# An eight-layer network on one core: one table of constants, two products of each attention unit on GpSimd, and the last step of the norms on ScalarE

## The chip, the cores and the metric

The kernel runs on one core of a Trainium2 chip. The time is device time in microseconds, the median of three runs. All arithmetic is in 32-bit floats, apart from some small bf16 operands of TensorE.

## The reference, cut to what matters

Four sequences of 1024 tokens with 128 features pass through eight layers. Each is `x = layernorm(x + layer(x))`, with mean and variance over the 128 features of a token:

- layer 0: cosine similarities within a sequence of 1024, counted and fed through a small map
- layer 1: a dense network whose weights are first binarised (sign times a mean)
- layer 2: an attention in each token between its 16 heads' channels; it is the largest part
- layer 3: a dense network with ternary weights and an inner norm
- layer 4: a gated linear recurrence; layer 5: four nested experts; layer 6: a state-space layer
- layer 7: a top-2 mixture of Kronecker-factored experts, whose tables are gathered by index

Layer 2 as the kernel computes it, for each token and head, with 64 channels as queries q, keys k and values v, and a running maximum m: `e = exp(q*k - m)`, summed over the keys a query may see, and `e*v` summed in the same way; the quotient is the output.

## The kernel before, in words

**Tiling.** The 4096 tokens are 32 tiles of 128 (`T`), in eight blocks of four tiles. For layers 3 to 7 the last block is split into two groups of two tiles, which makes nine groups (`SIZES`). Each tile gives layer 2 two *units* of 64 tokens, 64 units in all. A unit is laid out so that four partitions share the keys of a token, and its queries `qr` and maxima `mr` are copied into that layout by DMAs from SP's queue, issued in `prepare` (line 758). `qr` and `mr` have two buffers each.

**A unit of attention** is 17 pieces of e, which `feed` (line 817) starts in the order d1, n8 to n14, d0, n0 to n7. Piece nK has 32 x (60 - 4K) columns (n0 1920, n3 1536, n8 896), and d0 and d1 have 1024 each: 17408 columns a unit. Each piece takes room in a ring of 8768 columns (`ERING`), is handed out in order, and goes through six steps:

1. VectorE (DVE): e = q * k, with q from `qr` in SBUF and k from `kvr` in PSUM (in `feed`)
2. GpSimd (POOL): e = e - m (in `rest`, line 857)
3. ScalarE (ACT): e = exp(e)
4. TensorE (PE): sums of e into `acc` (`add_up(0)`)
5. DVE: e = e * v, in place, v from `kvr` in PSUM
6. PE: sums of e * v into `acc` (`add_up(1)`), after which the ring's room is free

`close` (line 910) turns `acc` into the layer's output and norm, once a unit.

**The other layers** run beside this. `chain_a` runs layers 0 and 1 (`front`, line 1710) of two blocks, then layers 3, 4 and 5 group by group, with the layers 0 and 1 of later blocks between; `chain_b` runs layer 6, `chain_c` layer 7. `norm` (line 528) ends layers 0, 1, 3, 4, 5 and 6: `stats` takes mean and variance on DVE and the reciprocal deviation `rs` on ACT, then one `tensor_scalar` on DVE for each tile of 128 columns reads PSUM and writes x; after it PE transposes x and ACT copies the transpose. It is called 52 times, for 192 tiles. Layer 2's norm is in `close` and layer 7's in `layer7`; both have code of their own.

**The order.** Each engine works through its instructions in the order in which they are written. That order is not in the source: every piece of work is a generator that says on which engine its next step goes and what it needs, and `Order` (line 109) picks the next step by a model of costs (`length`, line 65) and by ranks (`URGE`). A step of the other layers goes ahead of the attention's, unless its chain is ahead of its due place (`urge`, `LAG`). All instructions go through a recording helper, so all of them have line 52 in the profile and are told apart by tiles.

**The start.** `start` (line 382) loads 33 small constants and parameters by 37 DMAs, all on SP's queue, then `w0`, the biases and `Wo`. `fold` then loads layer 2's weights and folds a centring matrix `less` into them on PE and ACT. `layer0` of blocks 0 and 1 does `normalise` and `count` for both blocks together; `binarise` (line 622) comes next and writes layer 1's weights to DRAM scratch; then layer 1 of block 0, and with it the first unit can be prepared.

Of the kernel before, what the change touches and what calls it, by code (L numbers as in the profile page):

```python
# [14 lines left out]
AF = mybir.ActivationFunctionType  # L15
ALU = mybir.AluOpType
# [4 lines left out]
P = 128  # L21
NB, SEQ, D = 4, 1024, 128
NG = 8
TPG = 4
# [6 lines left out]
SH = S * H  # L31
ERING = 8768
LUMPS = 8
EPS = 0.05
ONE = 96
LAG = {"chain_a": (0.7, 300), "chain_b": (1.6, 290), "chain_c": (2.6, 132)}
# [249 lines left out]
class Model:  # L286
# [95 lines left out]
    def start(self):  # L382
        nc, a = self.nc, self.a
        load = {"ident": P, "rep": P, "SL": P, "U": P, "ex4": P, "ex2": P, "g4": 16, "g2": 32, "su": P, "sd": P, "par": 4, "iota": LUMPS,
                "blk": P, "less": P, "bz": 48, "route": 16, "beyond": R}
        par = {"f0_b1": 4, "f1_lnw": 4, "f1_lnb": 4, "a2_nw": 1, "f2_b1": 16, "f2_Wu": 1, "a0_W1": 1, "a0_b1": 1}
        wide = {"f2_bu": 1, "a3_bdt": 16, "a3_Alog": 16, "f3_sup": 1, "f3_sdn": 1}
        total = sum(load.values()) + sum(par.values()) + sum(wide.values()) + 64 + 32 + 128
        cst = self.keep([P, total], "cst")
        self.k, at = {}, 0  # L390

        def put(name, src, cols, bcast=False, rows=P):
            nonlocal at
            dst = cst[:, at : at + cols]
            self.k[name] = dst
            at += cols
            for r in range(0, P, rows):
                self.d.dma_start(dst[r : r + rows], src.to_broadcast([P, cols]) if bcast else src)

        put("ident", a["c_ident"], P)  # L400
        self.ident = self.k["ident"]
# [5 lines left out]
        self.v.memset(self.eps, LN_EPS)  # L407
        for g in (0, 1):
            self.load_x(g)
        for n, c in par.items():  # L410
            put(n, a[n], c)
        for n, c in load.items():
            if n != "ident":
                put(n, a["c_" + n], c)
        for n, c in wide.items():
            put(n, a[n], c, bcast=True)
        put("bup", a["f3_bup"], 64, rows=64)
        put("bdn", a["f3_bdn"], 32, rows=32)
        put("bd", a["c_bd"], 128)
        self.w0 = self.keep([P, 2, D], "w0")  # L420
# [107 lines left out]
    def norm(self, g, c, r):  # L528

        x = g.x  # L530
        mv, rs = yield from self.stats(r, c)
        for j in range(g.n):
            self.v.tensor_scalar(x[:, j, :], r[:, j, :], mv[:, j, 0:1], rs[:, j : j + 1], ALU.subtract, ALU.mult)
        self.drop(r)
        yield from self.transpose(g.xT, [x[:, j, :] for j in range(g.n)])
# [70 lines left out]

    def layer0(self, b):
        gs = self.blocks[2 * b : 2 * b + 2]
        for g in gs:
            if g.x is None:  # L610
                yield "SP", self.free("x")
                self.load_x(g.k)
            yield "ACT", self.free("xT")
            g.xT = self.new("xT")
        yield "ACT", self.free("ha")
        nT = self.new("ha")
        yield from self.together(*(self.normalise(g, nT) for g in gs))
        yield from self.together(*(self.count(g, nT) for g in gs))
        self.drop(nT)


    def binarise(self):

        self.w1 = []
        for half, n, count in ((0, 1, D), (1, 4, 512)):
# [24 lines left out]
            yield "SP"  # L650
            self.w1.append(self.keep([P, 512], "w1", pool=self.dram))
            self.d.dma_start(self.w1[half], wT)
            self.drop(wT)
# [52 lines left out]
    def fold(self):  # L706

        flat = self.Wkv.rearrange("p r v h n -> p (r v h n)")  # L710

        def piece(w, name, at):
            raw = yield from self.load("a", self.a[name][:, at : at + 512])
            yield "PE", self.free("bg")
            ps, dst = self.new("bg"), w[:, at : at + 512]
            self.pe.matmul(ps, lhsT=self.k["less"], rhs=raw, start=True, stop=True)
            yield "ACT"
            self.s.copy(dst, ps)
            self.drop(raw, ps)
            yield "SP"  # L720
            self.d.dma_start(dst[ONE : ONE + 1], self.a[name + "_b"][:, at : at + 512])

        yield from self.together(
            *(piece(w, name, at) for w, name, n in ((self.Wq, "a1_Wq", 2), (flat, "a1_Wkv", 4)) for at in range(0, 512 * n, 512))
        )
        self.folded = self.order.latest

# [30 lines left out]
    def prepare(self):  # L758

        flat = lambda tt: tt.rearrange("p h c -> p (h c)")  # L760
        for T in range(NG * TPG):
# [13 lines left out]
            for u in range(2):  # L775
# [12 lines left out]
                unit["uses"] = [9, 8]  # L788
                unit["subs"] = 17
                unit["ready"] = True  # L790
# [26 lines left out]
    def feed(self):  # L817
# [5 lines left out]
        count = 0  # L823
        for unit in self.units:
            for kind, i in order:
# [13 lines left out]
                else:  # L839
# [5 lines left out]
                    shape = lambda tt, nq=nq: tt.rearrange("p (a q) -> p a q", q=nq)  # L845
                yield "DVE", self.when(lambda: self.ering.can(SH * nq), lambda: self.ering.back(SH * nq)), True
                et = self.ering.take(SH * nq)
                e = shape(et)
                self.v.tensor_tensor(e, part(unit["qr"]), kk, ALU.mult)
                what = dict(first=(kind, i) == order[0], last=(kind, i) == order[-1], q0=q0, nq=nq, half=half)  # L850
                rest = self.rest(unit, count, kind, et, shape, part(unit["mr"]), vv, **what)
                self.order.spawn(rest, "rest", self.order.latest)
                count += 1
            self.drop(unit["qr"])
        self.retire("qr", "big", "a", "c")

    def rest(self, unit, count, kind, et, shape, m, vv, first, last, q0, nq, half):
        e = shape(et)
        rows = et.rearrange("p (s h q) -> p s h q", s=S, q=nq)

        def add_up(d):
            for hb in range(2):
                for s in range(S):
# [4 lines left out]
                    )  # L868

        yield "POOL"  # L870
        self.g.tensor_tensor(e, e, m, ALU.subtract)
# [838 lines left out]
    def front(self, b):  # L1710
        if b.k % 2 == 0:
            yield from self.layer0(b.k // 2)
        if b.k == 0:
            yield from self.binarise()
        yield from self.layer1(b)
# [62 lines left out]
    def run(self):  # L1778
# [13 lines left out]
        with self.tc.manual_schedule():  # L1792
            self.log_exp()
            self.order.spawn(self.fold(), "feed")
            self.order.spawn(self.prepare(), "prepare")
            for chain in (self.chain_a, self.chain_b, self.chain_c):
# [3 lines left out]
        assert not self.held and all(len(self.slots[k]) >= n for k, (n, _) in self.room.items()), self.slots  # L1800


URGE = {"close": 0, "prepare": 1, "chain_a": 2, "chain_b": 2, "chain_c": 2, "rest": 3, "feed": 4}
# [9 lines left out]
def arrays_of(i):  # L1813
# [63 lines left out]
    for n, s in (("up", "up"), ("dn", "down")):  # L1877
# [9 lines left out]
        "U": p <= q,  # L1887
        "rep": p % 32 == q % 32,
        "blk": (p % 16 == q % 16) / 8.0,
        "less": ((p == q) * 1.0 - (p == ONE)) * (q != ONE),  # L1890
        "bz": np.pad(p // 8 == np.arange(16)[None, :], ((0, 0), (16, 16))) * 8**-0.5,
# [11 lines left out]
    }  # L1903
    a.update({"c_" + n: c(np.asarray(v, np.float32)) for n, v in k.items()})
    return a
# [17 lines left out]
```

## Time and profile before

| | before |
|---|---|
| median of three runs | 4459.69 us (4457.38 to 4463.85) |
| the profiled execution's own time | 4459.83 us |
| its span, first to last instruction | 4458.1 us |
| DVE busy in the span | 3637.0 us |
| PE busy | 3532.0 us |
| POOL busy | 2697.3 us |
| ACT busy | 2443.8 us |
| first product of a unit on DVE starts at | 135.42 us |
| last product e * v of the last unit on DVE starts at | 3998.78 us |

The span falls into three stages: a start of 135 us, a long stage to about 4000 us in which the 64 units and the other layers run side by side, and an end of 458 us in which the layers of the last groups finish alone. "Busy" is the time in which an engine had an instruction in work; the idle time ahead of a group of instructions is put down to what ended last before it. A mean duration can count overlap with the next instruction; busy time divided by the count does not.

### The profile page before, as it was taken

The numbers are of one execution on the slowest core, as the hardware profiler recorded it, in microseconds if no ns is written. First come the engines' busy times: TensorE is split into PE (matmuls) and PEld (weight loads), VectorE is DVE, ScalarE is ACT, GpSimd is POOL, SyncE is SP. The second block draws the span as 40 slices with busy tenths as digits, with TensorE's granted clock in tenths as the row PEclk, the third lists the DMA queues.
The fourth block names the chain that finished last, engine by engine and source line by source line (L and its number), as shares of the span: only waits on it lengthen the run. The fifth ranks groups of instructions, "written<-read, shape, count | busy, mean of one in ns | idle before, by whom it ended". The sixth has DMA issues, their size and how long they took to land.

```text
span 4458.1 us, 91232 instructions
## 1 busy us (share of the span) xinstructions
PE 3532.0 (79%) x37044; PEld 1856.1 (42%) x37044; DVE 3637.0 (82%) x5143; ACT 2443.8 (55%) x4083; POOL 2697.3 (61%) x1254
## 2 busy tenths in 40 slices
PE   4567677788788888888788888988788888879973
PEld 2222224344344434444354434544354434437762
DVE  2899999899888998879979998779989998883421
ACT  3455555766446755657555655657555654555520
POOL 0598866776567775567756766557666775560111
PEclk8788889988899989989899888999998988998976
DMA  1221212212223232222323333133323223331555
GB/s 52 67 57 39 47 42 61 50 44 50 58 65 79 73 95 67 67 72 67 96 64 86 77 87 84 38 84 87 89 60 96 67 74 86 77 89 34 142 153 124
DMA packets 389933, 328.12 MB, mean 74 GB/s; under 512 B 201660, under 2 KB 325372, under 8 KB 389512
## 3 DMA queue, kind: packets, MB, share of 16 engines
q1 hardware_dynamic: 379016, 288.73, 26.3%
q0 software_dynamic: 10496, 33.56, 2.6%
q8 instruction: 290, 4.75, 0.5%
q14 instruction: 131, 1.07, 0.1%
HBM read 147.05 MB, written 40.89 MB: 42 GB/s over the span
## 4 chain that ended last, share of the span: by engine, by line
DVE 37%; PE 31%; issue 12%; POOL 9%; ACT 9%; DMA 2%; SPq 1%; DVEq 0%; POOLq 0%; ACTq 0%
DVE ringe L52 23%; PE bg L52 18%; PE acc L52 10%; POOL ringe L52 9%; DVE bg L52 5%; ACT ringe L52 4%; PE kvr L52 3%; SPq L52 1%; DVE a L52 1%; DVE x L52 1%; ACT ha L52 1%; DVE b L52 1%; DVE ast L52 1%; DVE t L52 1%; ACT b L52 1%
## 5 line engine op out<-in xcount | busy, mean ns | idle before, releaser
L52 POOL TENSOR_TENSOR ringe<-ringe,mr 128x1024 f32<-128x1024 f32 (+14 forms) x1088 | 2548.7, 2380 | 1150.5 <-DVE ringe L52 789.9
L52 PE MATMUL acc<-ringe,cst 128*32 128x256 f32 (+6 forms) x17418 | 1370.6, 428 | 509.2 <-ACT ringe L52 244.3
L52 ACT ACTIVATE ringe<-ringe 128x256 f32<-128x256 f32 (+14 forms) x962 | 997.6, 1053 | 790.2 <-POOL ringe L52 788.1
L52 DVE TENSOR_TENSOR ringe<-ringe,kvr 128x1024 f32<-128x1024 f32 (+14 forms) x1098 | 1289.8, 1204 | 129.9 <-PE acc L52 108.2
L52 DVE TENSOR_TENSOR ringe<-qr,kvr 128x1024 f32<-128x1024 f32 (+14 forms) x1088 | 1278.4, 1211 | 82.3 <-PE acc L52 45.7
L52 PEld LDWEIGHTS acc<-ringe,cst 128*32 128x32 f32 x17418 | 424.5, 115 | 1230.7 <-DVE ringe L52 467.6
L52 ACT ACTIVATE ringe<-ringe,cst 128x256 f32<-128x256 f32 x512 | 353.5, 771 | 106.7 <-POOL ringe L52 106.1
L52 PE MATMUL bg<-xT,a 128*128 128x512 f32 (+2 forms) x506 | 286.9, 675 | 34.8 <-DVE t L52 11.1
L52 PEld LDWEIGHTS bg<-b,b 64*128 64x128 f32 (+1 forms) x1650 | 178.8, 203 | 101.3 <-issue 42.6
L52 PE MATMUL bg<-b,b 64*128 64x128 f32 (+2 forms) x1650 | 202.2, 290 | 18.9 <-DVE b L52 5.5
L52 PE MATMUL kvr<-wkv,xT 128*32 128x256 f32 x2048 | 157.1, 430 | 48.4 <-DVE ringe L52 48.0
L52 PE MATMUL bg<-a,ha 128*128 128x128 f32 x1168 | 169.5, 291 | 12.8 <-ACT ha L52 12.8
L52 DVE TENSOR_TENSOR_SCAN bg<-lo,bg 128x512 f32<-128x512 f32 x128 | 155.4, 1217 | 22.2 <-ACT bg L52 22.2
L52 ACT COPY b<-bg 128x512 f32<-128x512 f32 (+2 forms) x245 | 106.7, 446 | 121.7 <-PE bg L52 119.8
L52 PEld LDWEIGHTS bg<-a,ha 128*128 128x128 f32 x1168 | 149.9, 201 | 24.9 <-ACT ha L52 14.5
L52 PEld LDWEIGHTS bg<-xT,a 128*128 128x128 f32 (+1 forms) x506 | 92.1, 213 | 159.1 <-issue 62.0
L52 ACT ACTIVATE ha<-bg,cst 128x512 f32<-128x512 f32 (+1 forms) x157 | 102.2, 665 | 79.8 <-PE bg L52 78.2
L52 POOL DMA_INDIRECT c<-in_f_tdn,elumps x22 | 20.8, 943 | 200.4 <-issue 196.0
L52 ACT ACTIVATE bg<-bg 128x512 f32<-128x512 f32 (+3 forms) x176 | 89.2, 509 | 75.8 <-PE bg L52 73.3
L52 ACT ACTIVATE b<-cst,five 128x128 f32<-128x128 f32 x412 | 129.5, 392 | 0.0
L52 DVE TENSOR_TENSOR b<-b,bg 128x256 f32<-128x256 f32 (+3 forms) x272 | 100.9, 401 | 34.0 <-PE bg L52 18.3
L52 PE MATMUL bg<-b,cst 128*128 128x512 f32 (+1 forms) x208 | 113.9, 634 | 0.5 <-ACT b L52 0.4
(598 smaller groups left out, 4641.5 us busy)
## 6 DMA issues: line engine op xcount, KB each, us to landing
qr<-q SPq DMA_DIRECT2D x512, 128.0 KB
mr<-t SPq DMA_DIRECT2D x512, 128.0 KB
a<-in_f_W SPq DMA_DIRECT2D x65, 256.0 KB
c<-in_f_Wdn SPq DMA_DIRECT2D x55, 256.0 KB
tu<-c SPq DMA_DIRECT2D x52, 256.0 KB
c<-tu SPq DMA_DIRECT2D x200, 64.0 KB
c<-td SPq DMA_DIRECT2D x98, 128.0 KB
td<-c SPq DMA_DIRECT2D x47, 256.0 KB
```

The costliest lines, as they stand in the source:

```text
L52: return f(*args, **kw)
```

## The change

**One table.** The constants and small parameters are laid side by side on the host in one array of 1475 columns, which two DMAs load: the identity matrix first, then the rest. The matrix `less` is loaded by `fold` on its own and given back.

**The order of the start.** `binarise` is a task of its own from the beginning; layer 1 waits until both its weights are written. `layer0` of the first pair still normalises both blocks, but counts only block 0; block 1's count comes when `chain_a` reaches block 1.

**Two shared products.** For pieces n8 and n3 of each unit, step 1 goes to POOL: ACT copies the 32 columns of k from PSUM to a small tile `ks` in SBUF, POOL multiplies q by it, and then subtracts m as before. `qr` is given back when the last of the 17 products is done, on whichever engine (`asked`).

**The last step of the norms.** In `norm`, DVE makes `nm = -mean * rs` from two small SBUF tiles (one `scalar_tensor_tensor` of up to four columns), and ACT applies scale and bias, one `activation` for each tile of 128 columns.

```diff
 def start(self):
-        load = {...}; par = {...}; wide = {...}
...
-        for n, c in par.items():
-            put(n, a[n], c)
...
-        put("bd", a["c_bd"], 128)
+        cst = self.keep([P, sum(CST.values())], "cst")
+        for name, cols in CST.items():
+            self.k[name] = cst[:, at : at + cols]
+            at += cols
+        self.load_x(0)
+        self.d.dma_start(cst[:, :P], a["cst"][:, :P])
+        self.load_x(1)
+        self.d.dma_start(cst[:, P:], a["cst"][:, P:])
...
 def norm(self, g, c, r):
         mv, rs = yield from self.stats(r, c)
+        nm = self.small([P, TPG], c + "nm")[:, : g.n]
+        self.v.scalar_tensor_tensor(nm, mv[:, :, 0], -1.0, rs, ALU.mult, ALU.mult)
+        yield "ACT"
         for j in range(g.n):
-            self.v.tensor_scalar(x[:, j, :], r[:, j, :], mv[:, j, 0:1], rs[:, j : j + 1], ALU.subtract, ALU.mult)
+            self.s.activation(x[:, j, :], r[:, j, :], AF.Identity, scale=rs[:, j : j + 1], bias=nm[:, j : j + 1])
...
 def layer0(self, b):
+        room = "ha" if b else "hc"
...
         yield from self.together(*(self.normalise(g, nT) for g in gs))
+        if b == 0:
+            yield from self.count(gs[0], nT)
+            return nT
         yield from self.together(*(self.count(g, nT) for g in gs))
...
 def feed(self):
-                yield "DVE", self.when(lambda: self.ering.can(SH * nq), lambda: self.ering.back(SH * nq)), True
+                shared = (kind, i) in SHARED
+                yield "ACT" if shared else "DVE", self.when(
+                    lambda: self.ering.can(SH * nq), lambda: self.ering.back(SH * nq)
+                ), True
...
-                self.v.tensor_tensor(e, part(unit["qr"]), kk, ALU.mult)
+                qk = part(unit["qr"]), kk
+                if shared:
+                    ks = self.small([P, SH], "ks", bufs=4)
+                    self.s.copy(ks, kk[:, :, 0])
+                    qk = qk[0], ks[:, :, None].to_broadcast(sh)
+                else:
+                    self.v.tensor_tensor(e, *qk, ALU.mult)
+                    self.asked(unit)
...
+    def asked(self, unit):
+        unit["asks"] -= 1
+        if unit["asks"] == 0:
+            self.drop(unit["qr"])
+            if unit is self.units[-1]:
+                self.retire("qr", "big", "a", "c")
...
 def rest(...):
+        if qk:
+            yield "POOL"
+            self.g.tensor_tensor(e, *qk, ALU.mult)
+            self.asked(unit)
         yield "POOL"
         self.g.tensor_tensor(e, e, m, ALU.subtract)
...
 def front(self, b):
         if b.k % 2 == 0:
-            yield from self.layer0(b.k // 2)
-        if b.k == 0:
-            yield from self.binarise()
+            self.nT = yield from self.layer0(b.k // 2)
+        elif b.k == 1:
+            yield from self.count(b, self.nT)
+            self.drop(self.nT)
+        yield "SP", self.when(lambda: len(self.w1) == 2)
         yield from self.layer1(b)
...
 def run(self):
+            self.w1 = []
+            self.order.spawn(self.binarise(), "chain_a")
...
+SHARED = ("n", 8), ("n", 3)
```

## The prediction

> **What bounds the kernel now.** I read first the busy times, then the same by stage, then the chain that ended last, then who waits for whom, and last the groups by shape.
>
> ```profile
> span 4458.1 us, 91232 instructions
> PE 3532.0 (79%) x37044; PEld 1856.1 (42%) x37044; DVE 3637.0 (82%) x5143; ACT 2443.8 (55%) x4083; POOL 2697.3 (61%) x1254
> ...
> DVE 37%; PE 31%; issue 12%; POOL 9%; ACT 9%; DMA 2%; SPq 1%; DVEq 0%; POOLq 0%; ACTq 0%
> ```
>
> The same in three stages (after the stage and its length: busy us of PE, PEld, DVE, ACT, POOL, then clock, DMA share, GB/s):
>
> ```profile
> 0.00:135.00 135.00, 69.52 (x258) 39.43 (x258) 35.20 (x93) 48.70 (x107) 3.41 (x9) 0.82 0.24 62
> 135.00:4000.00 3865.00, 3121.37 (x32117) 1546.01 (x32117) 3465.59 (x4567) 2242.98 (x3563) 2642.32 (x1189) 0.89 0.28 70
> 4000.00:4458.00 458.00, 341.11 (x4677) 270.61 (x4669) 136.21 (x485) 152.14 (x413) 51.53 (x56) 0.77 0.43 110
> ```
>
> In the long middle stage DVE is busy 3466 of 3865 us, 90%; PE 81%, POOL 68%, ACT 58%. DVE leads. What its 399 idle us wait for, and whom POOL waits for:
>
> ```profile
> DVE ringe L52 <- PE acc L52: 157.2, 126, 9.8
> DVE ringe L52 <- PE kvr L52: 39.3, 27, 3.5
> POOL ringe L52 <- DVE ringe L52: 789.9, 158, 20.4
> ```
>
> So POOL is fed by DVE and has room; PE is the engine that DVE waits for. DVE work taken out of this stage should shorten it, as far as PE lets it. Start and end are chains of short steps in which no engine is full.
>
> **The change, part 1: the start.** The chain in the start, in order of time:
>
> ```profile
> 21.70 4.20 DMA a<-in_a_Wq
> 25.95 5.46 PE bg L52 x10
> 35.48 12.84 PE bg L52 x40
> 87.83 5.67 PE bg L52 x8
> 135.43 1.21 DVE ringe L52
> ```
>
> The first weight is issued at 21.70 because 44 DMAs stand before it on SP's queue, 0.47 us each. In the changed order 11 stand before it: 0.74 + 11 x 0.47 = 5.9, and 4.2 to land gives 10.1 us. But the bytes ahead of it grow denser (some 2.5 MB; the stretch 4200 to 4300 moved 179 GB/s at a DMA share of 0.68, so 263 GB/s at full share, 9.5 us). I take 12.5: gain 13.4 us.
>
> From the first similarity product (36.94 in the timeline) to layer 1's first (87.83) are 50.9 us: the similarities of two blocks, then the binarising from 68.95 on. Afterwards there are 8 products of 0.86 us (6.9), then block 0's own steps, read off the same stretch: count 1.1, map on DVE 0.8, softplus on ACT 2.4 and DVE 0.7, PE 3.4, sum and statistics 2.3, deviation 0.6, norm 2.1, transposes 1.4, copy 0.6, with hops some 16.8. Together 23.7, gain 27.2. The binarising is costed at nothing: it took 18.9 us, starts at about 20 on the new scale and is hidden by these steps until about 47; were it late, layer 1 would wait for it.
>
> Block 1's count now lies between layer 1 of block 0 and the first unit, where block 1's layer 1 lay before (47.6 us in all): I charge 3 us. Sum: 13.4 + 27.2 - 3 = 37.6; the first product comes at 98 instead of 135.4. Some 8 us of DVE work of block 1 move into the middle stage.
>
> **Part 2: two products.** Rows of the two shapes, on DVE and, as a subtraction, on POOL:
>
> ```profile
> L52 DVE TENSOR_TENSOR ringe<-qr,kvr 128x1536 f32<-128x1536 f32 x64 | 111.6, 1744 | 8.8 <-PE acc L52 8.6
> L52 DVE TENSOR_TENSOR ringe<-qr,kvr 128x896 f32<-128x896 f32 x64 | 68.9, 1077 | 0.0
> L52 POOL TENSOR_TENSOR ringe<-ringe,mr 128x1536 f32<-128x1536 f32 x64 | 221.9, 3467 | 102.9 <-DVE ringe L52 70.0 <-PE acc L52 22.5 <-DVE cnt L52 5.3
> L52 POOL TENSOR_TENSOR ringe<-ringe,mr 128x896 f32<-128x896 f32 x64 | 135.0, 2109 | 34.5 <-DVE ringe L52 29.6 <-PE acc L52 4.7
> ```
>
> DVE loses 111.6 + 68.9 = 180.5 us. POOL gains, a product costed like a subtraction of the same shape, 221.9 + 135.0 = 356.9 us: 2999 in the middle stage, still below DVE. ACT gets 128 copies of 32 columns at 188 ns (the nearest row is a copy of 32 columns), 24 us, in an engine with 42% idle. A copy that waits for `kvr` would hold the exponentials behind it; the row of `kvr` above shows 3.5 us at most. `qr` is given back some 5 us later; DVE waited 3.3 us in all for the DMA that fills it, so the second buffer covers this. The piece stays about 2 to 4 us longer in the ring, which holds half a unit (30 us): free, as long as POOL isn't late.
>
> **Part 3: the norms.** 192 steps leave DVE:
>
> ```profile
> L52 DVE TENSOR_SCALAR x<-bg,amv,ars 128x128 f32<-128x128 f32 x124 | 42.3, 401 | 3.7 <-ACT ars L52 3.7
> ```
>
> Busy time by count is 341 ns; 168 of them lie in the middle stage, 57 us. In their place come 52 small operations nm, 47 of them there. The kernel has the same operation already, in layer 3:
>
> ```profile
> L52 DVE SCALAR_TENSOR_TENSOR anm<-amv,ars 128x4 f32<-128x4 f32 x7 | 6.2, 881 | 0.0
> L52 DVE SCALAR_TENSOR_TENSOR anm<-amv,ars x9: 148/156/2307, 567.9 to 4056.3; 128x4 f32<-128x4 f32 x7, 128x2 f32<-128x2 f32 x2
> ```
>
> Four columns take 156 ns at the median, but 881 on average and once 2307. The Trainium skill, "SBUF — State Buffer", section "Who interferes with whom", says why: a DVE instruction with two SBUF inputs shares a read port with GpSimd and waits until a GpSimd instruction that reads SBUF is over. `nm` has two SBUF inputs, the old step had one and PSUM. By the median the 47 cost 7 us, by the mean 41. POOL was 68% busy then and will be about 80%, so I take 0.9 us each, 42 us. The norms give DVE only 57 - 42 = 15 us, not 50.
>
> On ACT, x costs 192 steps with two pointer operands. The row of `ha<-ha,anm,ars` is 777 ns of busy time for 512 columns; less 384 columns at 0.83 ns (from ACT's 1920- and 128-column rows, 1805 and 304 ns) it is 0.45 us, so some 85 us in all. "ScalarE: Activation LUTs", section "Rules for kernel authors", tells one to keep such arithmetic on VectorE. Per step the rows agree, 0.45 against 0.34, which would make the sum 20 us worse if ACT were the full engine; at 58% it isn't, so by the trace this costs nothing. ACT then stands at about 64%. A norm's chain gets about 1 us longer (one more hop, slower steps); in the end stage there are four such norms: +4 us.
>
> **The sum,** against the profiled span of 4458.1. DVE in the middle stage: 3466 - 180.5 - 15 + 8 = 3278. Idle: 399 if nothing else changes. PE's share rises from 3121/3865 (81%) to about 3146/3728 (84%); waits that grow as load over free share rise by some 30%, and DVE's waits for PE above are 196, so +50: 450. The stage is 3728 (-137). Start 98, end 462: 4288. The profiled execution took 1.7 us more than its span, and is within 0.2 us of the median of the runs; predicted time **4290** (-3.8%).
>
> **Rivals.**
>
> DVE alone sets the pace. DVE's idle share stays 10.3%, or falls since POOL and ACT no longer make it wait: 3278/0.897 = 3654, or with 340 us of idle 3618; 98 + 3618 to 3654 + 462 is 4178 to 4214, say 4200. For it: POOL's 790 us of waiting for DVE. Against: PE's share.
>
> PE, or POOL beside it, takes the gain. If idle grows by 130 (DVE's waits for PE up by two thirds), the stage is 3807 and the time 4370. For it: PE is 31% of the chain, and the order is written from a model that doesn't know of the port. Against: PE's busy time holds waits within bursts of short products, and it reached 98% between 4100 and 4200.
>
> POOL becomes the bound, slower than before. POOL's work in the middle stage is 2999 us, 46.9 a unit; it idles 19.1 us a unit now (3865 - 2642, by 64). If this idle time stays, since a unit's pieces pass POOL one after another and wait for DVE between, a unit takes 66.0 us, the stage 4224, the time 4785. It decides where POOL's idle time stays above 14.0 us a unit (the stage then eats the 33 us net from start and end); my forecast needs 11.4. A mild form gives about 4490. Against: most of that idle time is waiting for DVE, which gets its work done sooner.
>
> The change does nothing to the middle stage: only start and end count, 4425.
>
> **How the numbers follow.** The forecast has 0.52 (its own range 4235 to 4330), DVE alone 0.18, PE or POOL taking the gain 0.17, the start alone 0.06, POOL as the bound 0.07. Leaving out the last two and the far edge of DVE's rival, some 0.2, the range is 4190 to 4395. Under 0.2% (9 us) a measurement of this kernel can't tell a change from none. Faster by more: 0.52 + 0.18 + 0.17 + most of 0.06 = 0.91; same 0.03; slower 0.06.
>
> **What would show it.** First product of a unit at about 98 us; DVE's middle stage at 3278 us of busy time and 88%; POOL near 3000 there with products of 2.1 and 3.5 us; nm at a mean near 0.9 us with a median far lower; ACT's x steps near 0.45. The prediction is wrong if POOL's products are slower than its subtractions, if nm costs 2 us, if DVE's waits for `acc` double, or if the first product comes after 120.

## The result, and the profile after

| | before | after | predicted |
|---|---|---|---|
| median (after: of 11 runs) | 4459.69 us | 4445.88 us (4429.67 to 4454.25) | 4290 |
| ratio to before, 95% interval | | 0.9967 (0.9956 to 0.9979) | 0.962 |
| span of the profiled execution | 4458.1 us | 4446.4 us | 4288 |
| start, to the first product | 135 us | 94 us | 98 |
| middle stage | 3865 us | 3916 us | 3728 |
| end | 458 us | 436 us | 462 |

The change gains 0.3%, just more than can be told from nothing, and the prediction of 3.8% was wrong. The start is as predicted. The middle stage, from which most of the gain was to come, is 51 us *longer* than before. First the page after (busy times and the chain that ended last), then its three stages (the stage and its length; busy us of PE, PEld, DVE, ACT, POOL; clock, DMA share, GB/s).

```profile
PE 3528.7 (79%) x37044; PEld 1877.8 (42%) x37044; DVE 3500.7 (79%) x4875; ACT 2520.3 (57%) x4403; POOL 2977.6 (67%) x1382
...
PE 28%; DVE 25%; issue 9%; POOL 8%; ACT 7%; DMA 1%; SPq 1%; DVEq 0%; POOLq 0%; ACTq 0%
```

```profile
0.00:94.00 94.00, 58.10 (x210) 32.79 (x210) 28.97 (x76) 44.03 (x107) 3.41 (x9) 0.83 0.28 80
94.00:4010.00 3916.00, 3132.67 (x32244) 1577.25 (x32244) 3340.15 (x4317) 2311.06 (x3848) 2922.61 (x1317) 0.88 0.28 68
4010.00:4446.00 436.00, 337.92 (x4590) 267.81 (x4590) 131.59 (x484) 165.20 (x449) 51.59 (x56) 0.82 0.46 121
```

In the middle stage DVE has 3340 us of work where it had 3466, so the relief is there, but it is idle for 3916 - 3340 = 576 us where it was idle for 399. The relief of 126 us has become idle time, and 51 us more beside it. (The chain can be followed here over 79% of the span only, so its shares don't compare with those of before.) What the waiting engines wait for, after:

```profile
POOL ringe L59 <- DVE ringe L59: 475.9, 118, 19.6
ACT ks L59 <- DVE ringe L59: 264.2, 88, 14.4
DVE ringe L59 <- PE acc L59: 253.4, 182, 9.6
POOL ringe L59 <- ACT ks L59: 241.8, 29, 28.6
```

POOL waits less for DVE (476 for 790), DVE more for PE (253 for 157), and the copy of the keys to `ks` waits 264 us in 88 stalls for DVE, which still reads the same `kvr`. The changed operations themselves, by shape and by tile:

```profile
L59 POOL TENSOR_TENSOR ringe<-qr,ks 128x1536 f32<-128x1536 f32 x64 | 177.4, 2772 | 171.1 <-ACT ks L59 157.9 <-ACT last L59 6.6 <-ACT bg L59 4.2
L59 POOL TENSOR_TENSOR ringe<-qr,ks 128x896 f32<-128x896 f32 x64 | 109.0, 1703 | 158.0 <-ACT ks L59 79.7 <-DMA qr<-q 48.2 <-PE bg L59 30.1
L59 DVE SCALAR_TENSOR_TENSOR anm<-amv,ars 128x4 f32<-128x4 f32 x36 | 34.4, 956 | 2.9 <-ACT ars L59 2.9
```

POOL's products cost 286 us, not 357; nm costs its 0.96 us on average. Sizes of this kind are not where 156 us went.

### The profile page after: what moved, and what is told of

Its sections match the earlier page's. It is cut to its first block, busy times and chain, and to the rows that moved or that the text cites. A ratio compares the mean times of both kernels' runs of the same rounds, so it can differ in the third digit from the quotient of the medians.

```text
span 4446.4 us, 91296 instructions
## 1 busy us (share of the span) xinstructions
PE 3528.7 (79%) x37044; PEld 1877.8 (42%) x37044; DVE 3500.7 (79%) x4875; ACT 2520.3 (57%) x4403; POOL 2977.6 (67%) x1382
## 4 chain that ended last, share of the span: by engine, by line
PE 28%; DVE 25%; issue 9%; POOL 8%; ACT 7%; DMA 1%; SPq 1%; DVEq 0%; POOLq 0%; ACTq 0%
PE bg L59 17%; DVE ringe L59 16%; PE acc L59 9%; POOL ringe L59 7%; DVE bg L59 4%; ACT ringe L59 3%; PE kvr L59 3%; ACT b L59 1%; ACT ha L59 1%; DVE t L59 1%; SPq L59 1%; DVE a L59 0%; ACT L59 0%; DVE ast L59 0%; DVE anm L59 0%
## 5 line engine op out<-in xcount | busy, mean ns | idle before, releaser
L59 PE MATMUL acc<-ringe,cst 128*32 128x192 f32 (+6 forms) x17412 | 1356.7, 428 | 501.4 <-DVE ringe L59 245.4
L59 ACT ACTIVATE ringe<-ringe 128x896 f32<-128x896 f32 (+14 forms) x964 | 1000.5, 1055 | 595.4 <-POOL ringe L59 592.8
L59 DVE TENSOR_TENSOR ringe<-qr,kvr 128x1024 f32<-128x1024 f32 (+12 forms) x960 | 1104.7, 1184 | 111.1 <-PE acc L59 66.3
L59 POOL TENSOR_TENSOR ringe<-qr,ks 128x896 f32<-128x896 f32 (+1 forms) x128 | 286.4, 2238 | 329.2 <-ACT ks L59 237.6
L59 PE MATMUL bg<-xT,a 128*128 128x512 f32 (+2 forms) x492 | 269.5, 656 | 33.3 <-ACT last L59 8.7
L59 PEld LDWEIGHTS bg<-b,b 128*128 128x128 f32 (+1 forms) x1628 | 191.1, 219 | 108.9 <-issue 48.2
L59 PE MATMUL bg<-b,b 64*128 64x128 f32 (+2 forms) x1628 | 214.8, 305 | 25.7 <-DVE b L59 7.6
L59 ACT COPY ks<-kvr 128x32 f32<-128x32 f32 x128 | 23.5, 184 | 264.5 <-DVE ringe L59 264.2
L59 DVE TENSOR_TENSOR b<-b,bg 128x256 f32<-128x256 f32 (+2 forms) x275 | 102.4, 402 | 47.1 <-PE bg L59 24.7
```

What stands on the lines that cost most here:

```text
L59: return f(*args, **kw)
```

## The experiments

The kernels ran on several chips. Each ratio is to the kernel before on the same chip, whose medians there were 4452 to 4479 us. Times read from a trace are not corrected for the chip; the two kernels' own traces come from one on which the kernel before takes 4460 us. Two kinds of experiment follow: in the first four and in those with another window the planner wrote a new order for the kernel; in the others every instruction kept its place, and only what it computes, or the engine that it is issued to, was altered. That difference turned out to be the main thing.

### Parts of the change, each planned afresh

The changed kernel with the norms on DVE again (`e1_norms_dve`):

```diff
-        self.v.scalar_tensor_tensor(nm, mv[:, :, 0], -1.0, rs, ALU.mult, ALU.mult)
-        yield "ACT"
         for j in range(g.n):
-            self.s.activation(x[:, j, :], r[:, j, :], AF.Identity, scale=rs[:, j : j + 1], bias=nm[:, j : j + 1])
+            self.v.tensor_scalar(x[:, j, :], r[:, j, :], mv[:, j, 0:1], rs[:, j : j + 1], ALU.subtract, ALU.mult)
```

> The changed kernel with the last step of the norms back on VectorE, as before; the table and the two shared products stay. Theory A (ScalarE stands still in order while the copy of k to ks waits for VectorE's products that read the same PSUM tile; this holds up the exponentials and gives back what the shared products saved): still about the changed kernel's time, 4430 to 4450 us, with 240 us or more of ScalarE's waiting before ks. Theory B (the norms on ScalarE do the harm: nm blocked on VectorE's port, ScalarE waiting for nm): 4330 to 4380 us. Theory C (a busier GpSimd holds VectorE's small two-input operations and becomes late): 4430 to 4450 us as well.

Measured: 1.0044 (1.0025 to 1.0063).

The changed kernel without the shared products (`e2_no_shared`), and without either move, which leaves the table and the early start (`e3_table_only`, with the first diff as well):

```diff
-SHARED = ("n", 8), ("n", 3)
+SHARED = ()
```

> The changed kernel without shared products (all 17 products of a unit on VectorE again); the table and the norms on ScalarE stay. Theory A: the start's gain shows, and the norms are worth little, 4400 to 4425 us. Theory B: the norms eat the start's gain, 4445 us or more. Theory C: 4400 to 4425 us.

> The table of constants and the new order of the start alone; products and norms as before. If the start's 41 us carry through to the end: 4415 to 4425 us. If an earlier start is given back later, since block 1's work now falls into the full stage: 4440 to 4460 us. All theories agree here; it gives the ground for the other runs.

Measured: 0.9898 (0.9873 to 0.9924) and 1.0008 (0.9997 to 1.002).

The copy to `ks` made as soon as PE has written `kvr`, before DVE reads it (`e4_ks_early`; the lines that then take this `ks` for the product are left out here):

```diff
+            for kind, i in SHARED:
+                if i // 8 == half:
+                    yield "ACT"
+                    ks = self.small([P, SH], "ks", bufs=4)
+                    self.s.copy(ks, ps[:, 0].rearrange("p s h n -> p (s h) n")[:, :, i % 8])
+                    unit["ks"][i] = ks
```

> The changed kernel with the copies of k to ks made as soon as TensorE has written kvr, ahead of VectorE's first product from it, and not in the middle of the products. Theory A: ScalarE's wait before ks falls from 264 us to under 60, and the time to 4300 to 4350 us. Theories B and C: the wait falls, but the time stays within 1% of the changed kernel's, 4420 to 4450 us.

Measured: 0.9956 (0.9943 to 0.997). The copy now waits for PE instead of DVE, and POOL hardly for the copy:

```profile
ACT ks L59 <- PE kvr L59: 74.2, 51, 6.0
POOL ringe L59 <- ACT ks L59: 57.5, 4, 28.4
```

The most conspicuous new wait, 264 us, is gone, and the ratio is only 0.1% lower, within the intervals (and in an order of its own). None of the three theories came out: A falls with this run (4458 us for 4350 at most), B with the norms put back, which made the kernel slower and not faster (4496 us for 4380 at most), and C had that run at 4450 at most. Taken at face value these four say that the table gains nothing, that the norms gain about 1%, and that the shared products cost 0.4 to 0.7%. The next experiments show that they can't be taken so: the table alone, for one, has its first unit finished 39 us earlier than the kernel before and its last only 11 us earlier (on a chip on which the kernel before takes 4478 us; by proportion, some 17 of the missing 28 us can be the chip's).

### The same work in another order

One number of the planner, the window in which two starts count as equal, is altered. Nothing else changes: same instructions, other order (`f5_before_replanned`, `f6_before_replanned2` with 0.04, `f4_after_replanned`, `f7_after_replanned2` with 0.04; `g1_no_shared_replanned` and `k2_table_replanned` do it to the kernels of the last section).

```diff
-EPS = 0.05
+EPS = 0.06
```

> The kernel before with one number of its planner altered, the window in which two starts count as equal (0.05 to 0.06 us): the same instructions in another order. Shows how much the time moves by the order alone. If the changes of 0.3 to 1 per cent seen so far are a matter of the order, this differs from the kernel before by as much, 0.99 to 1.01; if they come from the work moved, it stays within 0.3%.

> The kernel before with that window at 0.04 us: the same instructions in a third order. If the order moves the time at random, within 0.98 to 1.015 and neither at 1.0 nor at the 0.983 of the window of 0.06; if only one of the two orders was out of the common, this agrees with the other within 0.4%.

> The changed kernel with the planner's window for equal starts at 0.06 us in place of 0.05: the same instructions in another order. The kernel before went to 0.983 by this alone. If the order moves the time by 1 to 2% at random, this may lie anywhere from 0.975 to 1.01; if the window of 0.06 is better in itself, it is near 0.98; if the change is truly bound by what it moved, it stays at 0.997.

> The changed kernel with the planner's window for equal starts at 0.04 us: the same instructions in a third order. The three orders of the kernel before gave 1.0, 0.994 and 0.983, two of the changed kernel 0.997 and 0.990. If the change is worth nothing beyond the order, this is between 0.98 and 1.0, and the means of three agree within 0.5%; if it gains something that the order hides, it is below 0.983.

> The changed kernel without the shared products (table of constants and norms on ScalarE alone), planned with the window of 0.06 us. With the window of 0.05 it took 0.990, and the kernel before went from 1.0 to 0.983 by the window. If the two add, 0.973 to 0.978, the best of all kernels that do the whole work; if the order's effect is at random, 0.98 to 1.0.

> The kernel before with the table of constants alone, planned with the window of 0.06 us. With 0.05 it took 1.001, though its start is 39 us earlier. If the earlier start adds to the order that the kernel before got with 0.06 (0.983), this is 0.974 to 0.976. If every edit draws a new order, anywhere from 0.975 to 1.0, and the 0.983 was that one order's.

Measured, with the window of 0.05 beside them (each against the kernel before with 0.05):

| | 0.04 | 0.05 | 0.06 |
|---|---|---|---|
| before | 0.9943 (0.9927 to 0.996) | 1 | 0.9834 (0.9808 to 0.986) |
| after | 0.9995 (0.9981 to 1.001) | 0.9967 (0.9956 to 0.9979) | 0.9898 (0.9865 to 0.9931) |
| table alone | | 1.0008 (0.9997 to 1.002) | 0.9772 (0.9738 to 0.9806) |
| table and norms | | 0.9898 (0.9873 to 0.9924) | 0.9884 (0.9868 to 0.9901) |

The order alone moves the kernel before by 1.7%, five times the measured effect of the change, and turns its sign: planned with 0.04 or 0.06, the changed kernel is 0.5 to 0.7% *slower* than the kernel before. Over the three windows the kernel before averages 0.9926 and the changed one 0.9953: that the change came out faster with 0.05 was the luck of the order. With 0.05 and with 0.06 the edits rank differently. The table alone with 0.06 takes 4359.88 us and is faster than both kernels. Its page, beside that of the kernel before with 0.06 (first fence), shows how little of this the busy times tell:

```profile
PE 3494.0 (79%) x37044; PEld 1859.9 (42%) x37044; DVE 3645.3 (83%) x5143; ACT 2439.6 (55%) x4083; POOL 2699.2 (61%) x1254
```

```profile
PE 3472.5 (80%) x37044; PEld 1856.3 (43%) x37044; DVE 3647.3 (84%) x5143; ACT 2440.6 (56%) x4083; POOL 2699.5 (62%) x1254
```

DVE, ACT and POOL are busy as before to within some 10 us. Only PE's busy time differs, and with it the clock, to which I come back.

### Is the early start worth its 41 us?

The changed kernel in its own order, with six fills of the ring ahead of DVE's first work (`k1_late_start`):

```diff
+        for _ in range(6):
+            nc.vector.memset(self.ering.ap, 0.0)
```

> The changed kernel in its own order with six fills of the ring added on VectorE ahead of its first work (7.4 us each), so that the first product starts some 41 us later, at about 135 us, where the kernel before has it. If the earlier start is worth what the prediction gave it, this is 38 to 41 us longer than the changed kernel: 1.005 to 1.006 of the kernel before. If the lead is taken up within the first units, because these run against GpSimd in the changed kernel and against the fronts in both, it is 0.997 to 1.0.

Measured: 1.0086 (1.0058 to 1.0114), 1.2% or 53 us more than the changed kernel, give or take some 13. The fills delay the first product by 49 us. The copies that close a unit, in the changed kernel and in this one (durations, then the first and the last start):

```profile
L59 ACT COPY t<-acc x64: 984/1012/1042, 158.9 to 4012.3; 128x1024 f32<-128x1024 f32 x64
```

```profile
L59 ACT COPY t<-acc x64: 986/1012/1051, 208.8 to 4064.7; 128x1024 f32<-128x1024 f32 x64
```

Unit 0 is 50 us late and unit 63 is 52 us late. (The second trace comes from a chip on which the kernel before takes 4479 us, so some 17 of the 52 can be the chip's, by proportion; the ratio has no such share.) Little or nothing takes the delay up on the way. With the window of 0.06 the reverse is seen, where the table's lead lasts (the kernel before, then the table alone):

```profile
L52 ACT COPY t<-acc x64: 984/1012/1014, 201.7 to 3955.1; 128x1024 f32<-128x1024 f32 x64
```

```profile
L59 ACT COPY t<-acc x64: 984/1012/1033, 164.4 to 3917.6; 128x1024 f32<-128x1024 f32 x64
```

37.3 us of lead at unit 0, 37.5 at unit 63. (The trace of the kernel before is the slowest of its four runs; by the ratios, 0.9834 and 0.9772, the table gains 28 us there, give or take some 19.) As closely as these runs can tell, an earlier start is worth its length; in the changed kernel with 0.05 something else took it back.

### What a microsecond of each engine is worth, the order held

In `f2_dve_less` and the two after it, a part of three pieces' work is left out of the kernel before, on one engine; in `f1_pool_free` nearly all of the shared products is left out of the changed kernel. The planner still sees the whole work.

```diff
-        self.v.tensor_tensor(e, e, vv, ALU.mult)
+        if kind == "n" and i < 3:
+            few = [t[:, :SH // 2] for t in (e, e, vv)]
+            self.v.as_if("tensor_tensor", (e, e, vv, ALU.mult), (*few, ALU.mult))
```

> The kernel before, every instruction in its place, but VectorE's product of exponential and value is computed for half of the heads in three of a unit's n steps; the other half of these products is left out. VectorE loses some 193 us of its 3466 us and no other engine gains or loses work. If VectorE is the bound of the middle stage, as the prediction took it, the time falls by nearly all of that: 0.957 of the kernel before. If these instructions are worth their share of the chain of waits (23% of the span against 58% busy, 40%), 77 us: 0.983. If another engine sets the end, 0.995 to 1.0.

```diff
-                    self.pe.matmul(unit["acc"][at : at + 32, d, :, q0 : q0 + nq], ..., rhs=rows[...], ...)
+                    if kind == "n" and i < 3:
+                        out, rhs = out[:, :, : nq // 2], rhs[:, :, : nq // 2]
+                    self.nc.tensor.matmul(out, rhs=rhs, **how)
```

> The kernel before, every instruction in its place, but TensorE's sums of the products run over half of the columns in the same three n steps; the other half of the sums is left out. TensorE loses some 209 us of matmul time. If VectorE is the bound, 0.995 to 1.0. If TensorE is the bound, 0.953. If the two share the chain by the page (28% of the span on 79% busy, 35%), 74 us: 0.984.

```diff
-        self.g.tensor_tensor(e, e, m, ALU.subtract)
+        less = kind == "n" and i < 3
+        if less:
+            few = [t[:, : SH // 2] for t in (e, e, m)]
+            self.g.as_if("tensor_tensor", (e, e, m, ALU.subtract), (*few, ALU.subtract))
...
-            self.s.activation(et, et, AF.Exp)
+            self.s.activation(et, et, AF.Exp, scale=1e-3 if less else 1.0)
```

> The kernel before, every instruction in its place, but GpSimd subtracts the maximum for half of the heads in three of a unit's n steps (the other half of these subtractions is left out, and the exponentials of these steps are scaled down so that they stay finite). GpSimd loses some 190 us of its 2697 us, with no work moved to another engine. If GpSimd has room, as the prediction said (idle a third of the stage), 0.995 to 1.0. If its time is as dear as VectorE's (the kernel before with 165 us less on VectorE took 0.981, a half of that), 0.975 to 0.985.

```diff
+        nc.vector.memset(self.ering.ap, 0.0)
...
-            self.g.tensor_tensor(e, *qk, ALU.mult)
+            few = [t[:, :, 0:1] for t in (e, *qk)]
+            self.g.as_if("tensor_tensor", (e, *qk, ALU.mult), (*few, ALU.mult))
```

> The changed kernel, with every instruction in its place, but each of GpSimd's shared products computes only the first of a head's columns (32 of 896 or 1536 per partition); the rest of these products is left out. GpSimd gets back some 250 us of its 286 us of products, VectorE keeps its relief of 174 us, and the waits for the copied keys stay. If the added work on GpSimd is what ate the gain of the shared products, this falls well below the changed kernel's 0.997 of the kernel before: to 0.985 if the relief of VectorE is worth its share of the chain (40% of 174 us are 70 us, of which the later copies keep some), to 0.96 if VectorE alone bounds the stage as the prediction said. If it was the copy of the keys or the order of the work, it stays at 0.992 to 0.998.

| left out | ratio | busy time of the engine | time | time per us of busy time |
|---|---|---|---|---|
| on DVE, in the kernel before | 0.9807 (0.9791 to 0.9823) | 3637.0 to 3472.5 | -86 us | 0.52 |
| on PE, in the kernel before | 1.0011 (0.9998 to 1.0025) | 3532.0 to 3457.1 | +5 us | none |
| on POOL, in the kernel before | 0.9903 (0.9886 to 0.9919) | 2697.3 to 2335.3 | -43 us | 0.12 |
| POOL's products, after | 0.9794 (0.9778 to 0.9811) | 2977.6 to 2730.3 | -77 us against after | 0.31 |

(The times are the ratios' distances by 4458 to 4479 us.) DVE, busy for nine tenths of the stage, is worth half of its time in this order, not all of it. POOL, busy for two thirds, is not free. (Its cut was twice what was expected, 362 us for 190; DVE's was 165 for 193.) It is worth an eighth in the kernel before and, with the products on it, nearly a third, which is the answer that the last expectation asked for: it was the work added on POOL, not the copies of the keys, that ate the gain of the shared products, since the copies and their wait are all still there:

```profile
ACT ks L63 <- DVE ringe L63: 290.9, 91, 14.8
```

A part of POOL's figures is DVE's: with POOL relieved, DVE's own busy time falls as well, from 3500.7 to 3458.2 us (of which 7.4 are a fill of the ring that only this run has), and in the kernel before from 3637.0 to 3608.0. With that taken off at 0.52, an estimate, POOL alone is worth 0.08 and 0.21. The pages of the two runs, the kernel before with less on POOL first:

```profile
PE 3515.1 (79%) x37044; PEld 1855.8 (42%) x37044; DVE 3608.0 (81%) x5143; ACT 2438.7 (55%) x4083; POOL 2335.3 (53%) x1254
```

```profile
PE 3518.1 (81%) x37044; PEld 1872.1 (43%) x37044; DVE 3458.2 (79%) x4876; ACT 2510.7 (57%) x4403; POOL 2730.3 (63%) x1382
```

The nm row of the second says where some of DVE's 42 us are: 751 ns on average where it was 956.

```profile
L63 DVE SCALAR_TENSOR_TENSOR anm<-amv,ars 128x4 f32<-128x4 f32 x36 | 27.0, 751 | 2.6 <-ACT ars L63 2.6
```

The run on PE is a case of its own. The lines of the sums and of the commonest other matmuls, first before, then with the sums cut:

```profile
L52 PE MATMUL acc<-ringe,cst 128*32 128x256 f32 (+6 forms) x17418 | 1370.6, 428 | 509.2 <-ACT ringe L52 244.3 <-DVE ringe L52 234.2 <-ACT t L52 18.0
L52 PE MATMUL bg<-xT,a 128*128 128x512 f32 (+2 forms) x506 | 286.9, 675 | 34.8 <-DVE t L52 11.1 <-DMA a<-w 6.6 <-ACT last L52 5.1
```

```profile
L870 PE MATMUL acc<-ringe,cst 128*32 128x256 f32 (+6 forms) x17408 | 1240.4, 401 | 541.6 <-ACT ringe L52 262.2 <-DVE ringe L52 249.7 <-ACT t L52 15.1
L52 PE MATMUL bg<-xT,a 128*128 128x512 f32 (+2 forms) x506 | 294.3, 690 | 40.6 <-DVE t L52 13.4 <-DMA a<-w 6.5 <-ACT last L52 5.4
```

130 us leave the sums, but the other matmuls, which are untouched, get slower, and PE as a whole loses 75. The granted clock averaged 0.848 over these runs, against 0.876 for the kernel before on the same chip. So this run doesn't show that PE's time is worth nothing; the clock took a part of the relief back.

### The two moves, the order held

The changed kernel in its own order, with the moved instructions issued on DVE at the same places: the products (`h1_products_back`), the norms (`h2_norms_back`), and both (`h3_both_back`). `only_plan` tells the planner of an instruction and doesn't issue it.

```diff
-                    self.s.copy(ks, kk[:, :, 0])
+                    self.s.only_plan("copy", ks, kk[:, :, 0])
...
-            self.g.tensor_tensor(e, *qk, ALU.mult)
+            self.g.only_plan("tensor_tensor", e, *qk[:2], ALU.mult)
+            self.v.real.tensor_tensor(e, qk[0], qk[2], ALU.mult)
```

> The changed kernel, every other instruction in its place, but the two products of a unit are VectorE's again, at the place in the order where GpSimd's stood, read from the matmul's own output, without the copy of the keys. If relief of VectorE is what counts, as the prediction said, this is slower than the changed kernel by VectorE's 174 us at their share of the chain (40%): 70 us, 1.012 of the kernel before. If GpSimd's time is as dear as the run with its products left out says (77 us for 250 us, so some 88 us for the 286), the two nearly cancel and this is 0.992 to 0.995. If both engines' loads are worth nothing and the order decides, 0.997.

```diff
-        self.v.scalar_tensor_tensor(nm, mv[:, :, 0], -1.0, rs, ALU.mult, ALU.mult)
+        self.v.only_plan("scalar_tensor_tensor", nm, mv[:, :, 0], -1.0, rs, ALU.mult, ALU.mult)
+        for j in range(g.n):
+            self.v.real.tensor_scalar(x[:, j, :], r[:, j, :], mv[:, j, 0:1], rs[:, j : j + 1], ALU.subtract, ALU.mult)
         yield "ACT"
         for j in range(g.n):
-            self.s.activation(...)
+            self.s.only_plan("activation", ...)
```

> The changed kernel, every other instruction in its place, but the last step of the norms is VectorE's again (57 us) and the step for the bias (34 us) and ScalarE's four instructions are gone. If the move of the norms is worth the 0.8 to 1.1% by which kernels planned afresh with and without it differed, this is 1.005 to 1.008 of the kernel before. If that difference was the order's, this stays within 0.3% of the changed kernel: 0.994 to 1.0.

> The changed kernel in its own order with both the two products and the last step of the norms on VectorE again: of the change only the table of constants and the earlier start are left, and the order that was planned for the whole change. If the steps add (products 0.18%, norms 0.12%), this is 0.999 to 1.001 of the kernel before; as its first product is still some 41 us early, and the delayed start cost its whole delay, the order itself then costs about 40 us. If the two moves hinder each other, it is below 0.996.

Measured: 0.9985 (0.9973 to 0.9996), 0.9979 (0.9966 to 0.9992) and 1.0069 (1.0049 to 1.0089). Against the 0.9967 of the changed kernel, each move beside the other gains 0.1 to 0.2%, and both together 1.0%. So they don't add: most of the gain comes with whichever is made first, if the three ratios may be compared that closely. (They come from different chips; by the bare medians, 4475, 4475 and 4487 against 4446, the single moves would be worth 29 us each.) The expectations of the first (1.012, or 0.992 to 0.995) and of the third (0.999 to 1.001) were missed. The stages of this third kernel, which has the order and the start of the change and neither of the two moves:

```profile
92.00:4054.00 3962.00, 3181.37 (x32244) 1589.01 (x32243) 3479.47 (x4568) 2236.33 (x3551) 2644.16 (x1189) 0.86 0.27 68
4054.00:4488.00 434.00, 334.15 (x4592) 264.82 (x4590) 135.62 (x493) 159.10 (x433) 51.54 (x56) 0.83 0.47 122
```

Here the missing time shows. With DVE's load as before (3479 us for 3466), POOL's as before (2644 for 2642) and no copy of keys, the middle stage is 97 us longer than before. DVE waits 231 us for PE in it, most of the rise that the changed kernel showed:

```profile
DVE ringe L62 <- PE acc L62: 231.4, 169, 9.8
```

From this kernel to the changed one DVE loses 3479 - 3340 = 139 us of busy time in the stage, and the stage 3962 - 3916 = 46 us.

The 97 us need not be the price of the new order in itself. That order was made for products on POOL and norms on ACT, and runs here with both on DVE. The table alone in an order of its own (`e3_table_only`) is a matched one:

```profile
95.00:3990.00 3895.00, 3122.34 (x32032) 1559.47 (x32036) 3465.41 (x4547) 2239.09 (x3543) 2643.26 (x1189) 0.88 0.27 68
```

3895 us is 30 more than before, on a chip on which the kernel before takes 19 us more, and its end takes 487 us for 458. So most of the 97 us come with this order run on this work, and not with the new start. For the same reason the 1.0% that both moves gain in it is not their worth in general: with each kernel in an order of its own they gain 0.4% at the window of 0.05 (1.0008 to 0.9967) and lose 1.3% at 0.06 (0.9772 to 0.9898).

## Why the prediction was wrong

The profiled spans add up by steps, from before by way of the third kernel above to after: start 135 to 92, -43; that kernel's order in the middle stage, +97; in the end, 458 to 434, -24; the two moves in the middle stage, -46; the rest of the two moves, +4 (start 94, end 436). Together -12, from 4458 to 4446. By another way the steps would have other sizes.

**The step that failed first: DVE's relief taken at three quarters of its value, and POOL's added work at nothing.** The prediction put it as "DVE in the middle stage: 3466 - 180.5 - 15 + 8 = 3278. Idle: 399 if nothing else changes", with 50 added for PE. That is 137 us of stage for 188 us of relief, and the 357 us added to POOL were costed at nothing. Measured were 126 us of relief from before to after, and 46 us of stage for the 139 us that separate the changed kernel from its own order without the moves: a third. Three reasons show in the runs. A DVE microsecond is worth 0.52 by the run with less DVE work, in spite of DVE's 90%. A part of the relief comes back as slower small operations on DVE (under "Products" below). And the moved work is not gone. It costs POOL 279 us (2644 to 2923), and by the two POOL runs this is worth 0.12 to 0.31 a microsecond, 33 to 86 us. Against 0.52 x 139 = 72 us for DVE that is between a gain of 39 and a loss of 14; the 46 us measured lie a little outside, so these prices are rough. For the products alone, beside the norms on ACT, they fit: 0.52 x 108 = 56 us less those 33 to 86, where 0.18% or 8 us were measured. The statement "POOL is fed by DVE and has room" read the 790 us for which POOL waited as free time. But each piece goes through both engines in turn, and a longer step on POOL makes the piece late for ACT, PE and the ring: ACT waited 894 us for POOL in the kernel before, its longest wait, and the prediction passed over that line:

```profile
ACT ringe L52 <- POOL ringe L52: 894.3, 558, 14.9
```

In the changed kernel, with the order held, cutting POOL's products takes this wait from 717 to 544 us. (The sum of a wait is not a price either: from before to after it fell, and the stage got longer.)

**The step that wasn't there: the order.** The sum held the order of the rest constant. The planner writes it anew from modelled costs after every edit. The three orders of the kernel before span 1.7%, the two of the table alone 2.4%, so a prediction of such an edit that doesn't know the order can hardly be surer than about 1%. The prediction's range, down to 4190 and up to 4395, had no term for that.

**The rest, by its own steps.**

- Start: 98 us predicted, 94 found. Right in its steps too: the first weight is there at 11.3 us for 12.5, and from the first similarity product (21.03) to layer 1 (44.71) are 23.7 us for 23.7. By the delayed start it is worth its length, within the 13 us of that run.
- Products: DVE's two rows are gone, 180.5 us. But with the order held, DVE's busy time falls by only 108 us when they leave it, from the 3608.8 us of `h1_products_back` below to 3500.7. The rest comes back in small operations that get slower once POOL has the products, nm from 628 to 956 ns on average. The prediction had no such term for the products. POOL's price was a quarter too high, 357 against 286 us: a product with `ks` takes 2772 ns where the subtraction of that shape takes 3463.

```profile
PE 3559.2 (79%) x37044; PEld 1882.0 (42%) x37044; DVE 3608.8 (81%) x5003; ACT 2502.2 (56%) x4275; POOL 2700.9 (60%) x1254
```

- Copies: 24 us of ACT, right. "3.5 us at most" of waiting was wrong, it is 14.4 at most and 264 us in all: the row of `kvr` showed waits for PE, and the copy waits for DVE's readers of the tile. The early copy speaks against its mattering to the time, as far as two different orders can.
- Norms: nm at 0.96 us for the 0.9 taken, x at 0.46 for 0.45. The costs are right. The relief was 8 us of DVE (3509.1 to 3500.7, with the order held) for 15. One wait for POOL can outlast a single instruction, which the prediction's reading did not allow for: the longest nm of this trace ends at 1351.53 us, when a run of four subtractions on POOL does (start, duration):

```profile
1341.42 10.09 POOL L59 TENSOR_TENSOR ringe<-ringe,mr 128x1280 f32<-128x1280 f32 x4
1343.86 7.67 DVE L59 SCALAR_TENSOR_TENSOR anm<-amv,ars 128x4 f32<-128x4 f32 x1
```

What the norms are worth in time, 0.1% beside the products and perhaps more without them, can't be told more closely.
- DVE's stage: 3340 for 3278. Other small operations got dearer as well, which the prediction charged to nm alone. The counts `cnt` went from 428 ns each to 1886; 1236 of that is reached in the change's order with the products still on DVE, so only the rest is the products'.

```profile
L59 DVE TENSOR_TENSOR cnt<-c 128x4 f32<-128x4 f32 x8 | 15.1, 1886 | 15.4 <-ACT bg L59 15.4
```

- End: 462 predicted, 436 found, and 434 with the moves undone, so the 24 us come with the order.

Of the rivals, "the change does nothing to the middle stage" (4425) came nearest, by luck and not for its reason: the stage is moved by +97 and by -46. POOL as the bound is not what happened. POOL's idle time stayed at 15.5 us a unit (3916 - 2923, by 64), above the 14.0 that the rival named, and the stage did get longer; but it is longest (3962) where no work has been moved to POOL. The rival's mechanism is at work only as the price of 0.31.

**What stays open.** Why the stage is 97 us longer in the third kernel is not settled: the order as such and its misfit to the work were not separated. DVE's longer waits for PE and PE's own time go along with it (3181 us of busy time in the stage for 3121; some 20 of the 60 are 127 matmuls moved in from the start and the end, the rest goes with a clock of 0.86 for 0.89). Which comes first was not tried.

## What to carry to other kernels

Where four engines pass pieces to each other, price a microsecond moved by what a microsecond less on each engine gains *with the order held*, here 0.52 on VectorE and 0.12 to 0.31 on GpSimd (in these orders, at one size of cut each), and not by the busiest engine's busy time; a wait of the receiving engine is not a free slot. Where a planner writes the order, first measure what the order alone does, by altering a number that should not matter, and test parts of a change with every other instruction in its place. A larger wait in the list, like the 264 us of the copy, is a cause only once its removal has moved the time.

## What the runs showed of the hardware that was not expected

**The clock.** TensorE's busy time follows the granted clock: 3472.5 us at 0.886, 3494.0 at 0.881, 3532.0 at 0.875, 3571.7 at 0.861, for the same 37044 matmuls; the product of the two is 3075 to 3091 in these four. The clock differs by kernel, and it goes with the time: within the 23 runs of the kernel before on one chip, 0.01 of clock (they lie between 0.87 and 0.882) goes with 23 us, with a correlation of -0.93; on another chip, 37 runs, with 15 us and -0.52; three more sets of runs lie between 10 and 22 us. At some 20 us for 0.01, the third kernel's 0.861 against 0.877 would account for 32 us, and the 0.886 of the table alone with 0.06 against 0.877 for 18 us less. This is an association, and it can run the other way, since the same work in a shorter time is denser on PE. What makes one order keep a higher clock was not tried. The Trainium skill, "TensorE: Matmul & The Clock Gate", section "Part 1: The HAM clock gate", says that activity releases the throttle and idleness brings it back. The run with PE's sums cut fits that, with less PE work and the clock down from 0.876 to 0.848; that idle gaps are the cause is not shown here.

**A product is cheaper than a subtraction on GpSimd:** 1.80 ns a column against 2.25 at 1536 columns, 1.90 against 2.36 at 896. The product reads one operand from 32 columns and writes to another place, the subtraction works in place on two full ones; which of these it is was not separated.
